# A decoder layer on one core: the queries and keys of its second attention normed and rotated in pairs

## The chip, the cores and the metric

The kernel runs on one core of a Trainium2 chip. The metric is the device time of one launch, in microseconds. Before the change, three runs took 2617.15, 2618.02 and 2619.67 us, median 2618.02 us.

## The reference, cut to what matters

One layer of a decoder: a retention attention, a layer norm, a second attention over a long context and the own tokens, a layer norm, a gated feed-forward, a layer norm. All is float32. There are 8 batches of 100 tokens, the model is 1024 wide, the context has 722 tokens per batch. The change concerns the first lines of the second attention:

```python
q = (x @ wq).reshape(B, L, NUM_HEADS, HEAD_DIM)      # 16 heads of 128
k = (x @ wk).reshape(B, L, NUM_KV_HEADS, HEAD_DIM)   # 4 heads of 128
v = (x @ wv).reshape(B, L, NUM_KV_HEADS, HEAD_DIM)
q = rms_norm(q, q_norm_w)      # q * rsqrt(mean(q*q) + eps) * w
k = rms_norm(k, k_norm_w)
...
q = q * cos + rotate_half(q) * sin    # rotate_half: concat([-x2, x1])
k = k * cos + rotate_half(k) * sin
k_full = jnp.concatenate([k_ctx, k], axis=1)
...
out = jnp.einsum('bhlm,bmhd->blhd', probs, v_full)
```

## The kernel before, in words

**Layout.** Features lie on the 128 partitions, tokens along the columns. The 800 tokens are worked in two halves of 400 columns (4 batches of 100). A float32 number is split in two parts, hi and lo (`split2`, lines 68 to 70: ACT copies hi, DVE subtracts to get lo), and each product is three matmuls (`mm3`, lines 87 to 90: hi by hi, hi by lo, lo by hi). A projection (`proj`, line 102) is 8 k tiles of three matmuls, 24 in all, into one bank of PSUM. Banks have tags: three of "a", four of "s", one of "v"; the projections of this stage take "a" and "s" by turns (`acc_tag`).

**Stages.** First the retention attention (from line 308), then its output projection and layer norm (`out_proj`, whose result z1 is made half by half), then the stage of the change (lines 397 to 424), then the attention over the context (from line 427, "big", "kall" and "kss" are tiles of it), its output projection, and the feed-forward.

**The stage of the change.** A loop over four kv heads; each has four blocks of queries (i = 0 to 3), one of keys (4) and one of values (5), loaded as weights in groups of two to four (`load_w`, line 72: a DMA, an ACT cast and a DVE subtraction of 1024 columns). Every block is projected for both halves: 48 projections, 40 of them queries and keys. For such a one, lines 413 to 423 do:

- the square of the accumulator (ACT, tile sq, L414);
- its sum over the partitions, on GpSimd (`all_red`, L125, a PARTITION_ALL_REDUCE from sq to ss);
- the rotation (`rope`, lines 128 to 138) on DVE: the accumulator by the cosines (L134, from PSUM), the upper and the lower 64 partitions by the sines, written to the other half (L135, L136, both from PSUM), and the sum (L137);
- the inverse root (`inv_root`, lines 112 to 121): logarithm, exponential and square on ACT (L115, L116, L118) and two steps on DVE (L119, L120);
- the scaling by it (DVE, L419), and the split (ACT L69, DVE L70) to d, from which a DMA of 400 KB stores it in DRAM (L423).

Values are copied by ACT (vt, L143), transposed by TensorE (L146), split and stored. The accumulator's bank is free when L414 and L134 to L136 have read it.

**What sets the order.** All instructions of an engine run in one order, waiting by semaphores. The order is made when the program is built: a scheduler that follows a model of the engines' times places each instruction on its engine, so that operations of neighbouring projections are interleaved. All DMAs here are issued from SP's queue, also in one order. Pools give the tiles of the stage two buffers (three for d, one for vs and vt); a tile waits until its buffer has been read.

Of the kernel before, what the change touches and what calls it, by code (L numbers as in the profile page):

```python
# [8 lines left out]
F32 = mybir.dt.float32  # L9
# [7 lines left out]
P = 128  # L17
B, T, D = 8, 100, 1024
NB = 4                 # batches in a half
N = NB * T             # tokens in a half  # L20
KT = D // P            # k tiles of the model width
QT = KT // 2           # k tiles in one of the four big tiles
SC, SH = 722, 362      # context tokens per batch, and in the first half of it
SN = [SH, SC - SH]
NC = 7                 # chunks of keys: SC of the context, then T own ones
ORDER = (6, 5, 0, 1, 2, 3, 4)
C5 = SC - 5 * P        # context keys in chunk 5
R6 = SC + T - 6 * P    # keys in chunk 6
T6 = T - R6            # first token that sees keys of chunk 6
N6 = 4 * R6            # scores of chunk 6, of the tokens that see its keys  # L30
NH1 = 8                # heads of the first attention
NKV = 4                # kv heads of the second
NHID = 32              # blocks of the hidden width
UNITS = NHID // 2      # pairs of hidden blocks
LAST = 3               # pairs of the last down projection
CUT = 5 * T            # tokens in the first of the two parts that are normed last
# [5 lines left out]
def decoder_layer(ctx, tc, xT, cT, w1, wo1, w2, wo2, wc, w3, wd, gw, qw, kw, trig, dec, mask, out):  # L42
# [21 lines left out]
    def split(dst, src):  # L64
        """dst[:, 0] + dst[:, 1] == src, each with the 12 significant bits that one pass takes."""
        split2(dst[:, 0], dst[:, 1], src)
# [44 lines left out]

    def inv_root(pool, ss, eps, n=N):
        """-2 (ss + eps)^-1/2: by exp(-ln/2), then a Newton step."""
        r = pool.tile([P, n], F32, tag="r0", name="r0")
        nc.scalar.activation(r, ss, AF.Ln, bias=eps)  # L115
        nc.scalar.activation(r, r, AF.Exp, scale=-0.5)  # L116
        q = pool.tile([P, n], F32, tag="r1", name="r1")
        nc.scalar.activation(q, r, AF.Square)  # L118
        nc.vector.scalar_tensor_tensor(q, ss, eps, q, ALU.add, ALU.mult)  # L119
        nc.vector.scalar_tensor_tensor(q, q, 3.0, r, ALU.subtract, ALU.mult)  # L120
        return q
# [6 lines left out]
    def rope(pool, acc, cosw, sinw, tag="t1"):  # L128
        """acc * cos + (acc with its halves swapped) * sin."""
        t1 = pool.tile([P, N], F32, tag=tag, name=tag)  # L130
        t2 = pool.tile([P, N], F32, tag="t2", name="t2")
        a = bt(acc)
        h = P // 2
        nc.vector.tensor_tensor(bt(t1), a, cosw[:, None, :].to_broadcast([P, NB, T]), ALU.mult)  # L134
        nc.vector.tensor_tensor(bt(t2[0:h]), a[h:P], sinw[h:P, None, :].to_broadcast([h, NB, T]), ALU.mult)  # L135
        nc.vector.tensor_tensor(bt(t2[h:P]), a[0:h], sinw[0:h, None, :].to_broadcast([h, NB, T]), ALU.mult)  # L136
        nc.vector.tensor_tensor(t1, t1, t2, ALU.add)  # L137
        return t1

    def tokens_first(pool, acc):  # L140
        """[128, 4 x 100] -> PSUM [100, 4 x 128]: the transposes of the four batches."""
        vt = pool.tile([P, N], F32, tag="vt", name="vt", bufs=1)
        nc.scalar.copy(vt, acc)  # L143
        tr = bank("s")
        for b in range(NB):
            nc.tensor.transpose(tr[0:T, b * P:(b + 1) * P], vt[:, b * T:(b + 1) * T], ident)  # L146
        return tr[0:T]

# [1 line left out]
    o1d = dr.tile([NH1, P, 2, 2, 2, N], FR, name="o1d")            # head, p, half, block, hi/lo, token  # L150
# [42 lines left out]
    def load_constants(p, trg):  # L193
# [6 lines left out]
        # rotary tables with the norm weights of q and k; factors left over from inv_root  # L200
# [3 lines left out]
        nc.vector.tensor_scalar(tk, trg[:, 2:4], wts[:, 3:4], None, ALU.mult)  # L204
        return dcy

# [1 line left out]
    def out_proj(half, w, load_o, res, yp, ybufs, p, make_z, dst, after=None):  # L208
        """res + o @ w of one half, then its layer norm: split for the next products, and to dst."""
# [71 lines left out]
    # A norm with little left to do once the last block of rows is there: all blocks are taken relative to the mean  # L281
    # of the others, so that the mean of what they then hold, delta, is that of the last block alone, and the
    # variance is mean(y^2) - delta^2 (delta^2 is at most an eighth of mean(y^2)).
# [24 lines left out]
    with sbuf("l1", 2) as p:  # L308
# [17 lines left out]
        for h in range(NH1):  # L326
# [14 lines left out]
            # scores with their decay, and o^T  # L341
# [21 lines left out]
            # a block of the context weights, split once for all batches  # L363
# [33 lines left out]
    kapool = sbuf("ka", 2, "right")  # L397
    ka = kapool.__enter__()
    with sbuf("l2", 2) as p:
        for kv in range(NKV):  # L400
            for i0, i1 in ((0, 4), (4, 6)) if kv == 0 else ((0, 2), (2, 4), (4, 6)):
                ws = [load_w(w2[kv, i]) for i in range(i0, i1)]
                for half in range(2):
                    bs = slice(half * NB, (half + 1) * NB)
                    for i in range(i0, i1):
                        acc = proj(ws[i - i0], z1[half], tag=acc_tag())
                        if i == 5:
                            tr = tokens_first(p, acc).rearrange("p (b d) -> p b d", b=NB)
                            vs = p.tile([T, NB, 2, P], FR, tag="vs", name="vs", bufs=1)
                            split2(vs[:, :, 0], vs[:, :, 1], tr)  # L410
                            nc.sync.dma_start(out=f32(vd[kv, :, bs]), in_=f32(vs))
                            continue
                        sq = p.tile([P, N], F32, tag="sq", name="sq")
                        nc.scalar.activation(sq, acc, AF.Square)  # L414
                        ss = all_red(p, sq, "ss")
                        tb = tq if i < 4 else tk
                        t = rope(p, acc, tb[:, 0], tb[:, 1])
                        r = inv_root(p, ss, eps_k)
                        nc.vector.scalar_tensor_tensor(  # L419
                            t, t, -0.5 if i < 4 else -0.5 * math.sqrt(P), r, ALU.mult, ALU.mult)  # L420
                        d = p.tile([P, NB, 2, T], FR, tag="d", name="d", bufs=3)
                        split2(d[:, :, 0], d[:, :, 1], bt(t))
                        nc.sync.dma_start(out=f32(qd[kv, i, :, bs] if i < 4 else kd[kv, :, bs]), in_=f32(d))  # L423
    z1pool.__exit__(None, None, None)

# [1 line left out]
    y2pool = sbuf("y2", 1)  # L427
    y2p = y2pool.__enter__()
    with sbuf("cx", 2) as p, sbuf("c1", 1) as p1:
        for b in range(B):  # L430
# [10 lines left out]
            for kv in range(NKV):  # L441
                # K^T of the context, to be scaled by its norms when the scores leave PSUM, and V
# [29 lines left out]
                # -2 / norm of the context keys, keys on partitions  # L472
# [14 lines left out]
                # scores, keys on partitions, and their maximum  # L487
# [23 lines left out]
                # exponentials, split, and their sum  # L511
# [27 lines left out]
                # 1 / sum: exp(-ln), then a Newton step (the sum is 1 or more)  # L539
# [22 lines left out]
    # [C11 C12; C21 C22] = [A11 A12; A21 A22] [B11 B12; B21 B22] by Strassen's seven products; the rows of A  # L562
    # are two blocks of one weight, the columns of B the two halves of the tokens
# [60 lines left out]
    def w_pair(*ops):  # L624
        """Two of the sums of quarters of a weight, split; a sum goes to the first quarter's place unless that is kept."""
# [15 lines left out]
    def seven(i, part, t0=None):  # L641
        """Two blocks of the gate (part 0) or of the other factor (part 1): C11, C12, C21, C22."""
# [24 lines left out]
        add(s2, s2, s4)                                     # C21  # L667
# [6 lines left out]
        add(s4, s4, prod(t2, 1, "b11+b12"))                 # C22  # L674
        m5 = prod(t3, 0, "b22")
        add(s1, s1, m5, ALU.subtract)                       # C11
        add(s3, s3, m5)                                     # C12
        return s1, s3, s2, s4

    # the first two blocks by all eight products: half of them need the first half of the tokens alone  # L680
# [13 lines left out]
    with sbuf("ff", 1) as p:  # L694
# [59 lines left out]
        # the last rows are normed in two parts  # L754
# [16 lines left out]
def _chunks(w, n):  # L771
    """[K, M] -> [M / 128, K / (n 128), 128, n 128]: k tiles of 128 x 128 side by side."""
    import numpy as np
    K, M = w.shape
    a = w.reshape(K // (n * P), n, P, M // P, P)
    return np.ascontiguousarray(a.transpose(3, 0, 2, 1, 4)).reshape(M // P, K // (n * P), P, n * P)
# [62 lines left out]
```

## Time and profile before

| what | value |
|---|---|
| median of three runs | 2618.02 us |
| span of the profiled execution | 2615.0 us |
| TensorE matmul busy | 2552.7 us, 98% |
| DVE busy | 1922.2 us, 74% |
| ACT busy | 1256.3 us, 48% |
| GpSimd busy | 466.3 us, 18% |
| mean granted TensorE clock | 0.992 |
| L125, all-reduce of sq to ss, 56 times (40 in the stage) | 157.3 us, 2817 ns mean |

The profile is of one execution. Its own time is its span, from the first to the last instruction, 2615.0 us; the runs that are timed without it lie 2.2 to 4.7 us above. The page divides the span in 40 slices of 65.4 us and gives a digit per slice, the busy share in tenths. Lines such as "L137 DVE TENSOR_TENSOR t<-t,t" name the line of the kernel, the engine, the operation, and the tiles written and read; then come how many there are, their busy time, the mean of one in ns, and the idle time of the engine ahead of them with what ended it. "PE" is TensorE's matmul, "PEld" its weight load.

### The profile page before, as it was taken

The numbers are of one execution on the slowest core, as the hardware profiler recorded it, in microseconds if no ns is written. First come the engines' busy times: TensorE is split into PE (matmuls) and PEld (weight loads), VectorE is DVE, ScalarE is ACT, GpSimd is POOL, SyncE is SP. The second block draws the span as 40 slices with busy tenths as digits, with TensorE's granted clock in tenths as the row PEclk, the third lists the DMA queues.
The fourth block names the chain that finished last, engine by engine and source line by source line (L and its number), as shares of the span: only waits on it lengthen the run. The fifth ranks groups of instructions, "written<-read, shape, count | busy, mean of one in ns | idle before, by whom it ended". The sixth has DMA issues, their size and how long they took to land.

```text
span 2615.0 us, 37589 instructions
## 1 busy us (share of the span) xinstructions
PE 2552.7 (98%) x14438; PEld 2511.4 (96%) x14438; DVE 1922.2 (74%) x3201; ACT 1256.3 (48%) x2202; POOL 466.3 (18%) x222
## 2 busy tenths in 40 slices
PE   8999999999998899999999999999999999999998
PEld 8999999999998899999999999999999999999996
DVE  4454554456999888888988989866866766866885
ACT  4555544533555455655655566533433433423351
POOL 0010000000544434434333343100000000000000
PEclk9999999999999999999999999999999999999999
DMA  5323333664434644544554553564421211211221
GB/s 173 98 98 119 100 117 122 214 241 154 144 133 138 236 158 137 188 158 146 174 166 139 185 173 113 210 245 143 146 73 65 73 57 65 81 50 64 70 84 51
DMA packets 157233, 346.44 MB, mean 132 GB/s; under 512 B 45018, under 2 KB 95578, under 8 KB 147838
## 3 DMA queue, kind: packets, MB, share of 16 engines
q1 hardware_dynamic: 157054, 344.05, 39.5%
q8 instruction: 113, 1.85, 0.3%
q14 instruction: 66, 0.54, 0.1%
HBM read 279.81 MB, written 64.19 MB: 132 GB/s over the span
## 4 chain that ended last, share of the span: by engine, by line
PE 80%; DVE 10%; ACT 6%; issue 3%; DMA 2%; SPq 0%; DVEq 0%; ACTq 0%
PE a L88 16%; PE a L90 16%; PE a L89 16%; PE s L88 8%; PE s L89 8%; PE s L90 8%; PE v L88 3%; PE v L90 2%; PE v L89 2%; DVE r L119 1%; ACT L116 1%; ACT L115 1%; PE s L469 1%; DVE ot L378 1%; DVE t L136 1%
## 5 line engine op out<-in xcount | busy, mean ns | idle before, releaser
L88 PE MATMUL a<-big,w 128*128 128x400 f32 (+2 forms) x2300 | 778.5, 339 | 17.1 <-ACT big L69 9.5
L89 PE MATMUL a<-big,w 128*128 128x400 f32 (+2 forms) x2300 | 779.7, 339 | 0.0
L90 PE MATMUL a<-big,w 128*128 128x400 f32 (+2 forms) x2300 | 778.3, 339 | 0.0
L88 PEld LDWEIGHTS a<-big,w 128*128 128x128 f32 x2300 | 432.4, 188 | 20.6 <-ACT big L69 9.8
L90 PEld LDWEIGHTS a<-big,w 128*128 128x128 f32 x2300 | 433.9, 189 | 0.6
L89 PEld LDWEIGHTS a<-big,w 128*128 128x128 f32 x2300 | 433.1, 188 | 1.1 <-DVE big L70 0.5
L69 ACT CAST w<-wst 128x1024 fp32r<-128x1024 f32 (+2 forms) x300 | 259.2, 869 | 346.6 <-PE a L90 152.6
L70 DVE TENSOR_TENSOR w<-wst,w 128x1024 fp32r<-128x1024 f32 (+2 forms) x300 | 303.7, 1015 | 164.8 <-ACT w L69 163.2
L125 POOL PARTITION_ALL_REDUCE ss<-sq x56 | 157.3, 2817 | 725.4 <-DVE sq L362 442.3
L459 POOL PARTITION_ALL_REDUCE kss<-ksq x64 | 171.6, 2682 | 141.2 <-ACT ksq L458 140.7
L69 ACT CAST w<-as 128x512 fp32r<-128x512 f32 x90 | 55.9, 621 | 215.3 <-PE a L90 180.9
L88 PE MATMUL s<-big,w 128*128 128x400 f32 x428 | 150.4, 352 | 2.5 <-ACT big L69 2.5
L89 PE MATMUL s<-big,w 128*128 128x400 f32 x428 | 149.4, 349 | 1.6 <-DVE big L70 1.6
L90 PE MATMUL s<-big,w 128*128 128x400 f32 x428 | 148.8, 348 | 0.0
L505 ACT ACTIVATE s<-s,rk 128x400 f32<-128x400 f32 x160 | 88.0, 591 | 97.3 <-DVE sm L527 63.3
L663 DVE TENSOR_TENSOR s<-s 128x400 f32<-128x400 f32 x183 | 102.4, 569 | 25.3 <-ACT s L659 19.5
L125 POOL PARTITION_ALL_REDUCE mb<-sm x32 | 83.3, 2603 | 201.1 <-DVE sm L527 201.1
L524 ACT ACTIVATE s<-s 128x800 f32<-128x800 f32 (+1 forms) x128 | 95.1, 750 | 41.0 <-DVE s L518 38.1
L70 DVE TENSOR_TENSOR pl<-s,ph 128x800 fp32r<-128x800 f32 (+1 forms) x128 | 108.3, 850 | 2.5 <-ACT ph L69 2.0
L506 DVE TENSOR_TENSOR mx<-mx,s 128x400 f32<-128x400 f32 x128 | 80.5, 629 | 26.5 <-ACT s L505 23.3
L88 PE MATMUL a<-z,w 128*128 128x400 f32 x192 | 70.5, 367 | 24.0 <-DVE t L136 22.9
L69 ACT CAST ph<-s 128x800 fp32r<-128x800 f32 (+1 forms) x128 | 92.4, 731 | 0.9
(269 smaller groups left out, 5605.6 us busy)
## 6 DMA issues: line engine op xcount, KB each, us to landing
wst<-in_w SPq DMA_DIRECT2D x137, 512.0 KB
w<-wcd SPq DMA_DIRECT2D x64, 1024.0 KB
wst<-in_wo SPq DMA_DIRECT2D x64, 512.0 KB
wst<-in_wd SPq DMA_DIRECT2D x32, 512.0 KB
o1d<-of SPq DMA_DIRECT2D x32, 400.0 KB
big<-o1d SPq DMA_DIRECT2D x16, 800.0 KB
qd<-d SPq DMA_DIRECT2D x32, 400.0 KB
q<-qd SPq DMA_DIRECT2D x32, 400.0 KB
```

The source lines that it names most:

```text
L69: nc.scalar.copy(hi, src)
L70: nc.vector.tensor_tensor(lo, src, f32(hi), ALU.subtract)
L88: nc.tensor.matmul(acc, lh, rh, start=start, stop=False)
L89: nc.tensor.matmul(acc, lh, rl, start=False, stop=False)
L90: nc.tensor.matmul(acc, ll, rh, start=False, stop=stop)
L115: nc.scalar.activation(r, ss, AF.Ln, bias=eps)
L125: nc.gpsimd.partition_all_reduce(y, x, P, op)
L459: nc.gpsimd.partition_all_reduce(ss[:, at], sq[:, at], P, RED.add)
L505: nc.scalar.activation(sc, sp, AF.Copy, scale=rk[:, c:c + 1])
L506: nc.vector.tensor_tensor(mx, s[:, 1] if j == 2 else mx, sc, ALU.max)
L524: nc.scalar.activation(e, e, AF.Exp)
L663: nc.vector.tensor_tensor(t, x, y, op)
```

## The change

The function `rope` is no longer used in this stage. A new function `normed` takes two projections at once: two query blocks of the same half of the tokens, or the two halves of the key block. The square and the product with the cosines are still made per projection, straight from PSUM; the swap of the halves is now two ACT copies of 64 partitions from PSUM to t2. All that follows works on 800 columns: the sum over the partitions, the product with the sines, the sum, the inverse root, the scaling and the split. For this the rows of the sine tables are swapped once at the start. Tiles sq, d, r0 and r1 of this stage have one buffer, ss, t1 and t2 two. The keys of both halves are stored by one DMA in place of two; for each query block there is one, as before. The order of loops and weights is as before, but that the keys of both halves come ahead of the first values. Comments were dropped as well, which shifts line numbers.

```diff
-    def inv_root(pool, ss, eps, n=N):
+    def inv_root(pool, ss, eps, n=N, bufs=None):
...
         nc.vector.tensor_scalar(tk, trg[:, 2:4], wts[:, 3:4], None, ALU.mult)
+        for t in (tq, tk):
+            sw = p.tile([P, T], F32, tag="sw", name="sw", bufs=1)
+            nc.vector.tensor_copy(sw, t[:, 1])
+            nc.vector.tensor_copy(t[0:P // 2, 1], sw[P // 2:P])
+            nc.vector.tensor_copy(t[P // 2:P, 1], sw[0:P // 2])
...
     with sbuf("l2", 2) as p:
+        def wide(tag):
+            return p.tile([P, 2, N], F32, tag=tag, name=tag, bufs=1 if tag == "sq" else 2)
+
+        def normed(accs, cosw, sinw, scale):
+            sq, t1, t2 = wide("sq"), wide("t1"), wide("t2")
+            h = P // 2
+            for i, acc in enumerate(accs):
+                acc = acc()
+                nc.scalar.activation(sq[:, i], acc, AF.Square)
+                nc.scalar.copy(t2[0:h, i], acc[h:P])
+                nc.scalar.copy(t2[h:P, i], acc[0:h])
+                nc.vector.tensor_tensor(bt(t1[:, i]), bt(acc), cosw[:, None, :].to_broadcast([P, NB, T]), ALU.mult)
+            ss = wide("ss")
+            nc.gpsimd.partition_all_reduce(ss, sq, P, RED.add)
+            b4 = t2.rearrange("p i (b t) -> p (i b) t", b=NB)
+            nc.vector.tensor_tensor(b4, b4, sinw[:, None, :].to_broadcast([P, 2 * NB, T]), ALU.mult)
+            nc.vector.tensor_tensor(t1, t1, t2, ALU.add)
+            flat = lambda t: t.rearrange("p i n -> p (i n)")
+            r = inv_root(p, flat(ss), eps_k, 2 * N, bufs=1)
+            nc.vector.scalar_tensor_tensor(flat(t1), flat(t1), scale, r, ALU.mult, ALU.mult)
+            d = p.tile([P, 2, NB, 2, T], FR, tag="d", name="d", bufs=1)
+            d4 = d.rearrange("p i b l t -> p (i b) l t")
+            split2(d4[:, :, 0], d4[:, :, 1], t1.rearrange("p i (b t) -> p (i b) t", b=NB))
+            return d
...
-                        sq = p.tile([P, N], F32, tag="sq", name="sq")
-                        nc.scalar.activation(sq, acc, AF.Square)
-                        ss = all_red(p, sq, "ss")
-                        tb = tq if i < 4 else tk
-                        t = rope(p, acc, tb[:, 0], tb[:, 1])
-                        r = inv_root(p, ss, eps_k)
-                        nc.vector.scalar_tensor_tensor(
-                            t, t, -0.5 if i < 4 else -0.5 * math.sqrt(P), r, ALU.mult, ALU.mult)
-                        d = p.tile([P, NB, 2, T], FR, tag="d", name="d", bufs=3)
-                        split2(d[:, :, 0], d[:, :, 1], bt(t))
-                        nc.sync.dma_start(out=f32(qd[kv, i, :, bs] if i < 4 else kd[kv, :, bs]), in_=f32(d))
+                    if i0 < 4:
+                        for j in range(i0, i1, 2):
+                            d = normed([lambda i=i: proj(ws[i - i0], z1[half], tag=acc_tag()) for i in (j, j + 1)],
+                                       tq[:, 0], tq[:, 1], -0.5)
+                            for i in range(2):
+                                nc.sync.dma_start(out=f32(qd[kv, j + i, :, bs]), in_=f32(d[:, i]))
+                        continue
+                    if half == 0:
+                        d = normed([lambda half=half: proj(ws[0], z1[half], tag=acc_tag()) for half in range(2)],
+                                   tk[:, 0], tk[:, 1], -0.5 * math.sqrt(P))
+                        nc.sync.dma_start(out=f32(kd[kv]).rearrange("p b l t -> p (b l t)"),
+                                          in_=f32(d).rearrange("p i b l t -> p (i b l t)"))
```

More of the change, by code (lines that the diff above doesn't have):

```diff
@@ L110, in ln_exp @@
         tc.keep_in_program_order(nc.scalar.preload_act_table_set(LN_EXP))
-    def inv_root(pool, ss, eps, n=N):
-        r = pool.tile([P, n], F32, tag="r0", name="r0")
+    def inv_root(pool, ss, eps, n=N, bufs=None):
+        r = pool.tile([P, n], F32, tag="r0", name="r0", bufs=bufs)
         nc.scalar.activation(r, ss, AF.Ln, bias=eps)
         nc.scalar.activation(r, r, AF.Exp, scale=-0.5)
-        q = pool.tile([P, n], F32, tag="r1", name="r1")
+        q = pool.tile([P, n], F32, tag="r1", name="r1", bufs=bufs)
         nc.scalar.activation(q, r, AF.Square)
@@ L404, in decoder_layer @@
                     bs = slice(half * NB, (half + 1) * NB)
[L405 to L412, printed above, removed]
-                        sq = p.tile([P, N], F32, tag="sq", name="sq")
-                        nc.scalar.activation(sq, acc, AF.Square)
-                        ss = all_red(p, sq, "ss")
-                        tb = tq if i < 4 else tk
-                        t = rope(p, acc, tb[:, 0], tb[:, 1])
-                        r = inv_root(p, ss, eps_k)
-                        nc.vector.scalar_tensor_tensor(
-                            t, t, -0.5 if i < 4 else -0.5 * math.sqrt(P), r, ALU.mult, ALU.mult)
-                        d = p.tile([P, NB, 2, T], FR, tag="d", name="d", bufs=3)
-                        split2(d[:, :, 0], d[:, :, 1], bt(t))
-                        nc.sync.dma_start(out=f32(qd[kv, i, :, bs] if i < 4 else kd[kv, :, bs]), in_=f32(d))
@@ L424, in decoder_layer @@
+                    tr = tokens_first(p, proj(ws[1], z1[half], tag=acc_tag())).rearrange("p (b d) -> p b d", b=NB)
+                    vs = p.tile([T, NB, 2, P], FR, tag="vs", name="vs", bufs=1)
+                    split2(vs[:, :, 0], vs[:, :, 1], tr)
+                    nc.sync.dma_start(out=f32(vd[kv, :, bs]), in_=f32(vs))
     z1pool.__exit__(None, None, None)
```

## The prediction

> **What bounds the kernel now.** First the page's 40 slices, to find the stage. The change touches the queries and keys of the second attention, which the records of tile d place at 671 to 904 us: slices 10 to 13, counted from 0.
>
> ```profile
> PE   8999999999998899999999999999999999999998
> DVE  4454554456999888888988989866866766866885
> PEclk9999999999999999999999999999999999999999
> ```
>
> TensorE is at 90% or more nearly everywhere, but not in slices 12 and 13, and there DVE is at 9. Next the busy time by stretches: TensorE's time and matmuls first, then TensorE loads, DVE, ACT and POOL, then the clock.
>
> ```profile
> 680.00:700.00 20.00, 15.26 (x71) 14.58 (x70) 19.73 (x36) 11.62 (x24) 12.06 (x5) 0.83 0.36 129
> 700.00:720.00 20.00, 20.00 (x113) 19.94 (x112) 19.66 (x33) 10.01 (x20) 8.33 (x3) 1.00 0.49 161
> 720.00:760.00 40.00, 37.36 (x199) 36.97 (x198) 39.51 (x61) 21.64 (x42) 18.97 (x7) 0.96 0.35 125
> 760.00:800.00 40.00, 40.00 (x223) 39.94 (x223) 39.44 (x56) 20.02 (x38) 18.76 (x7) 1.00 0.42 138
> 800.00:840.00 40.00, 32.94 (x169) 32.46 (x168) 39.55 (x58) 20.49 (x38) 17.13 (x7) 0.87 0.42 140
> 840.00:880.00 40.00, 30.95 (x161) 30.30 (x161) 39.65 (x61) 24.68 (x47) 18.09 (x8) 0.94 0.58 203
> ```
>
> DVE is full (98 to 99%), ACT at 54%. TensorE did 936 matmuls in these 200 us; at the pace of 760 to 800 (223 in 40 us) they take 168 us, so **32 us of TensorE are lost here**. The waits say to whom:
>
> ```profile
> PE a L88 <- DVE t L136: 22.9, 5, 7.1
> ```
>
> Five gaps, 22.9 us: a projection wants a PSUM bank that DVE has not read out (L136 is its last reader). The other 9 us are the half clock after gaps (means of 0.83 to 0.96). So DVE sets the pace of this stage. Its groups there (640 to 910 us), busy and mean ns of one:
>
> ```profile
> L137 DVE TENSOR_TENSOR t<-t,t 128x400 f32<-128x400 f32 x40 | 31.0, 777 | 0.1
> L119 DVE SCALAR_TENSOR_TENSOR r<-ss,eps_k,r 128x400 f32<-128x400 f32 x40 | 30.7, 767 | 0.1
> L419 DVE SCALAR_TENSOR_TENSOR t<-t,r 128x400 f32<-128x400 f32 x40 | 30.2, 758 | 0.4
> L70 DVE TENSOR_TENSOR w<-wst,w 128x1024 fp32r<-128x1024 f32 x21 | 30.2, 1443 | 1.6 <-ACT w L69 1.4
> L70 DVE TENSOR_TENSOR d<-t,d 128x400 fp32r<-128x400 f32 x40 | 27.3, 684 | 1.6 <-ACT d L69 1.2
> L135 DVE TENSOR_TENSOR t<-s,tq 64x400 f32<-64x400 f32 x16 | 9.2, 576 | 0.2
> ```
>
> Undisturbed, the timeline has 0.565 us (L137), 0.63 (L119), 0.57 (L419, d) and 1.22 (w). The excess is 8.4 + 5.5 + 7.4 + 4.6 + 4.5 = **30 us in which DVE was blocked**. By what, the timeline shows:
>
> ```profile
> 726.49 2.86 POOL L125 PARTITION_ALL_REDUCE ss<-sq  x1 [1.34 <-DVE r L119]
> 726.81 2.10 DVE L419 SCALAR_TENSOR_TENSOR t<-t,r 128x400 f32<-128x400 f32 x1
> ...
> 731.14 2.60 POOL L125 PARTITION_ALL_REDUCE ss<-sq  x1 [1.79 <-DVE r L119]
> 731.54 0.58 DVE L135 TENSOR_TENSOR t<-s,tq 64x400 f32<-64x400 f32 x1
> 732.15 1.16 DVE L70 TENSOR_TENSOR d<-t,d 128x400 fp32r<-128x400 f32 x1
> ```
>
> L419 takes 2.10 instead of 0.57 us under an all-reduce; L135, which reads PSUM, isn't touched; d is held until about 732.74 (end less 0.57), 1.6 us after the all-reduce began. So one all-reduce of 400 columns closes DVE for 1.6 of its 2.60 us to operations with both inputs in SBUF.
>
> [...]
>
> **The change, part by part.** 40 query and key projections become 20 pairs. Spacings from start to start count, since neighbours overlap (timeline of 725 to 735 us).
> - Before, DVE per projection: L134 0.58, L135 0.61, L136 0.60, L137 0.48, L119 0.55, L120 0.49, L419 0.49, split 0.49, together 4.29; per pair 8.58 us.
> - After: two cosine products from PSUM, 2 x 0.58; sine product, sum, L120's step, scaling and split at 800 columns, 5 x 0.90 (the spacing of L522); L119's step 0.55 + 0.41 = 0.96. Together 6.62. **Saved: 1.96 x 20 = 39 us.** Most of it is the swap of halves (2.42 per pair on DVE), replaced by one 800-column product.
> - ACT: per pair before 2 x (0.49 + 0.62 + 0.53 + 0.54 + 0.53) = 5.4; after 2 x 0.49, four 64x400 copies, 0.96 for the logarithm, 3 x 0.87 (L524 at 128x800). The copies from PSUM appear nowhere in this form: nearest is L143 (128x400, PSUM) at 0.49; bounds 0.39 (its spacing) and 0.60; taken 0.48. Sum 6.5: 21 us more ACT in a stage where it is at 54%, so about 64%. Its load hides; without that cover it would cost those 21 us.
> - POOL: 40 all-reduces of 400 columns become 20 of 800, and nothing in the trace has that size. L459's 362 and 360 columns take 2.38 to 2.46 us against 2.60 for 400: 0.14 to 0.22 us per 38 columns. So 800 take 4.1 to 4.9 us, their lock 1.6 + 1.5 to 2.3 us. Bounds: 1.6 (it doesn't grow) and 4.2 (whole instruction doubled, 5.2, less the 1.0 us tail). I take 3.2: [...]
> - How much of it hits DVE: 30 of 40 x 1.6 = 64 us before, since L134 to L136 (1.79 us) often ran under the lock. After, only 1.16 of 6.62 us per pair read PSUM, and the order of the built program puts the sine product first after the ACT copies, which follow the square that starts the all-reduce. So I take 2.5 of 3.2 us: 50 us, **20 us more than before**. Bounds 15 (lock 1.6, the same share, 47%) and 84 (4.2, all of it).
> - Waits: the sine product now heads DVE's queue and waits for ACT; behind it are the previous pairs' split, L119's step and both cosine products, which free the banks. The banks are "a" 3 and "s" 4, a new projection needs one about every 4.4 us, so a bank may be held some four projections, about 17 us. Some 6 us of delay (lock and three 0.9 us operations) is covered. Without that cover each pair would stop TensorE.
> - ACT's split cast waits for the scaling on DVE, and behind it stand the next squares, and the copy ahead of v's transposes, on which TensorE waits in order. In the built order one or two projections (4.4 us each) lie between; I cost it at nothing, up to 4 us for each of 8 v projections.
> - d, sq, r0 and r1 have one buffer: the next split waits for the previous pair's stores. A pair lasts 9 to 11 us; nothing.
> - DMAs: 32 query stores remain, key stores go from 8 to 4: 1.3 us of SP issue less, which has slack. Weight loads stand behind the stores in SP's queue as before, and their splits stay several pairs ahead of use.
> - The table's swap: six small DVE copies at the start, where DVE is at 63% and TensorE's order hardly changes: nothing, at most 1.3 us.
> - Outside this stage the built order is the same, but for a few matmuls and loads changing places.
>
> Sum: -39 + 20 = **-19 us**. Check: DVE's demand before is 40 x 4.29 + 24 weights x 1.14 + 5 (vs) + 7 (big) + 30 = 241 us, and the trace has 660.6 to 903.7, 243. After it is 222. TensorE needs 48 projections x 24 x 0.179 = 206 us and about 6 for the transposes. DVE stays the bound, by 10 us, and 13 of the 32 lost us stay lost. The next stage is TensorE's, so an earlier end stays won. The page gives the profiled execution's span as 2615.0; the median of the runs is 2618.0, 3.0 more, and the step is taken from it: 2618 - 19 = 2599.
>
> **Rivals.**
> 1. TensorE becomes the bound. If the locks fall on cosine products and DVE's idle time (15 to 30 us in all), all 32 us return: 2586. For it: TensorE works ahead during v projections, which need little DVE. Against: five of every six us per pair now have two SBUF inputs.
> 2. A wait takes the place of the old one: ACT's queue, held by the split cast, delays v's transposes by the 4 us of the bound: 8 x 4 = 32 us. In these stops DVE catches up, so the 13 us at the banks vanish, and 32 are lost as before: 2618. For it: ACT gets more work and more waits on DVE. Against: today that wait is 0.6 us on TensorE.
> 3. Slower: the 800-column all-reduce closes DVE longer. It decides where the block per pair passes (39 + 30) / 20 = 3.5 us. At the bound of 4.2 us, all of it hitting, DVE's sum is -39 + 54 = +15, and gaps bring more half clock: about 2633. For it: nothing here shows 800 columns. Against: the slope of the three sizes gives 3.1 to 3.9, and not all hits.
>
> **How the numbers follow.** Forecast (2590 to 2608) 0.45; rival 1 0.20; rival 2 0.13; rival 3 0.22. 0.2% is 5 us, about what a measurement of this kernel can tell from no change. Faster: 0.45 + 0.20 = 0.65; same 0.13; slower 0.22. The range runs from 2584 (all lost time back, 2 us spare) to 2622, the near end of rival 3; beyond it lie some 0.17 above and 0.03 below.
>
> **What would show it.** All-reduces near 4.2 us, each holding one DVE operation for 2 to 3 us; DVE still at 95% or more; the waits for banks down from 22.9 to about 10; tile d ending near 883 instead of 904. It is wrong if the all-reduce is over 5 us, if TensorE waits for vt, or if the gain sits outside this stage.

## The result, and the profile after

| | before | after |
|---|---|---|
| median of 20 runs each, same chip | 2616.68 us (2613.28 to 2620.59) | 2620.39 us (2617.84 to 2623.18) |
| span of the profiled execution | 2615.0 us | 2618.1 us |

The ratio is 1.0014 [1.0008, 1.0021]: the kernel became a little slower, where 2599 had been forecast. The change does what it says, but the stage takes as long as it did: the last record of tile d ends at 908.2 us, before at 903.7.

The slices of the kernel after, to be held against those of before:

```profile
PE   8999999999889999999999999999999999999998
DVE  4454554456899878889889989866866766866885
PEclk9999999999999999999999999999999999999999
```

TensorE still has its two poor slices; they have moved from 12 and 13 to 10 and 11. DVE had 9, 9, 9, 8, 8 in slices 10 to 14 and now has 8, 9, 9, 8, 7: it is a little less full, and TensorE isn't better fed for it. The stretches of the kernel after (TensorE, its loads, DVE, ACT, POOL, then the clock):

```profile
680.00:700.00 20.00, 14.89 (x82) 14.26 (x81) 19.07 (x14) 11.37 (x19) 10.88 (x2) 0.99 0.33 120
700.00:720.00 20.00, 16.92 (x86) 16.84 (x87) 18.58 (x19) 14.56 (x25) 9.25 (x2) 0.84 0.42 148
720.00:760.00 40.00, 38.27 (x209) 37.70 (x207) 39.31 (x33) 27.66 (x43) 19.86 (x5) 1.00 0.36 130
760.00:800.00 40.00, 33.13 (x174) 33.04 (x175) 33.77 (x32) 24.12 (x38) 13.96 (x4) 0.87 0.41 144
```

Between 760 and 800 us, TensorE's best stretch before (223 matmuls), both engines now stand idle for a part of it: 174 matmuls, and DVE at 33.8 of 40 us. The waits of the kernel after (us in total, times, longest):

```profile
ACT r L115 <- DVE r L120: 40.6, 14, 5.4
...
PE s L146 <- ACT vt L143: 20.2, 3, 7.4
...
PE a L88 <- DVE t L418: 9.4, 3, 7.8
DVE d L70 <- ACT d L69: 8.1, 8, 1.9
...
DVE t L418 <- ACT t L417: 6.0, 7, 1.7
```

The stops for a bank went from 22.9 to 9.4 us, as forecast. In their place TensorE stands 20.2 us, in three stops, at the transposes of v, for ACT's copy (0.6 us before). DVE now waits for ACT: 8.1 us for the split's cast (1.2 before) and 6.0 for the swapped copies. DVE's groups of the kernel after, busy and mean ns:

```profile
L120 DVE SCALAR_TENSOR_TENSOR r<-r,r 128x800 f32<-128x800 f32 x20 | 53.4, 2670 | 0.1
L422 DVE TENSOR_TENSOR t<-t,tq 128x800 f32<-128x800 f32 x16 | 32.8, 2049 | 0.0
...
L426 DVE SCALAR_TENSOR_TENSOR t<-t,r 128x800 f32<-128x800 f32 x20 | 22.9, 1143 | 0.1
L70 DVE TENSOR_TENSOR d<-t,d 128x800 fp32r<-128x800 f32 x20 | 21.4, 1069 | 8.2 <-ACT d L69 8.1
```

An operation on 800 columns takes 0.98 us undisturbed (L522 of the kernel before, at 128x800, has 0.975 in the median), and 0.91 from start to start (L426 and L422 of the kernel after, at 862.30 and 863.21), where 0.90 had been forecast. L120 and L422 have the same size and take 2.67 and 2.05 on average: the lock of the all-reduce now falls mostly on these two. One pair, from the timeline of the kernel after, shows the whole chain:

```profile
758.60 4.85 POOL L420 PARTITION_ALL_REDUCE ss<-sq  x1 [6.01 <-DVE r L119]
758.83 4.15 DVE L120 SCALAR_TENSOR_TENSOR r<-r,r 128x800 f32<-128x800 f32 x1
...
763.07 0.96 ACT L115 ACTIVATE r<-ss,eps_k 128x800 f32<-128x800 f32 x1 [2.58 <-DVE r L120]
...
764.81 0.86 ACT L69 CAST d<-t 128x800 fp32r<-128x800 f32 x1 [0.78 <-DVE t L426]
765.58 0.86 ACT L116 ACTIVATE r<-r 128x800 f32<-128x800 f32 x1
766.35 0.47 ACT L143 COPY vt<-s 128x400 f32<-128x400 f32 x1
...
766.87 1.09 PE L146 MATMUL s<-ident,vt 128*100 128x128 f32 x4 [7.39 <-ACT vt L143]
```

The all-reduce begins at 758.60; L120, 0.98 us of work, ends at 762.98, so DVE was let in at 762.00: the lock, from the start of the all-reduce to there, is 3.4 us of the 4.85. ACT stands behind L120 (r0 has one buffer), then behind the scaling; only at 766.35 does it copy v out of its bank, and TensorE, idle for 7.4 us, goes on at 766.87. One lock is thus passed on through DVE and ACT to TensorE. It isn't the whole stop: of the 7.4 us, ACT stands idle for 3.4 (2.58 and 0.78), and the other 4.0 are its own instructions that the order puts ahead of the copy, and the copy.

For the experiments one number is taken from each trace: **blocked time**, the durations of the DVE instructions between 660 and 912 us less what the same size takes undisturbed (0.57 us for 400 columns, 0.905 for the 720 and 724 of tile big, 0.985 for 800, 1.22 for 1024), where that excess is over 0.25 us. It is 30.7 us before and 58.7 after, good to about 1 us; in these two kernels every instruction that it counts overlaps an all-reduce.

### The profile page after: what moved, and what is told of

Read it like the earlier page. It is cut to its first block, busy times and chain, and to the rows that moved or that the text cites. A ratio compares the mean times of both kernels' runs of the same rounds, so it can differ in the third digit from the quotient of the medians.

```text
span 2618.1 us, 37344 instructions
## 1 busy us (share of the span) xinstructions
PE 2550.3 (97%) x14438; PEld 2510.2 (96%) x14438; DVE 1910.1 (73%) x3047; ACT 1285.7 (49%) x2202; POOL 465.1 (18%) x202
## 4 chain that ended last, share of the span: by engine, by line
PE 81%; DVE 9%; ACT 5%; issue 3%; DMA 2%; POOL 0%; SPq 0%; DVEq 0%; ACTq 0%; POOLq 0%
PE a L88 16%; PE a L90 16%; PE a L89 16%; PE s L88 8%; PE s L89 8%; PE s L90 8%; PE v L88 3%; PE v L90 2%; PE v L89 2%; DVE r L120 2%; DVE w L70 1%; DVE r L119 1%; PE s L498 1%; ACT L116 1%; ACT L115 1%
## 5 line engine op out<-in xcount | busy, mean ns | idle before, releaser
L88 PEld LDWEIGHTS a<-big,w 128*128 128x128 f32 x2300 | 433.4, 189 | 19.2 <-ACT big L69 9.2
L420 POOL PARTITION_ALL_REDUCE ss<-sq x20 | 108.3, 5417 | 284.8 <-DVE z L70 165.6
L125 POOL PARTITION_ALL_REDUCE ss<-sq x16 | 43.7, 2730 | 442.4 <-DVE sq L367 442.4
L125 POOL PARTITION_ALL_REDUCE mb<-sm x32 | 83.3, 2603 | 197.5 <-DVE sm L556 197.5
```

What stands on the lines that cost most here:

```text
L88: nc.tensor.matmul(acc, lh, rh, start=start, stop=False)
L125: nc.gpsimd.partition_all_reduce(y, x, P, op)
L420: nc.gpsimd.partition_all_reduce(ss, sq, P, RED.add)
```

## The experiments

Theory: the lock that an all-reduce puts on DVE is what the stage loses, before and after; the change took out of DVE's work the products from PSUM, which can run under the lock (L135 kept its 0.58 us there), and left what can't (L419 took 2.10 us for 0.57). Rival A: the single buffers of r0, r1, sq and d. Rival B: ACT's longer queue, by way of v's transposes. The expectations name them by these causes. One reservation holds for all: only pool_later keeps nearly the order of instructions of the kernel after. In the others the scheduler laid the stage out anew, so no run changes one thing with the order held fixed. Ratios are to the kernel before, on the same chip.

| kernel | median us | ratio [95%] | blocked us |
|---|---|---|---|
| before_no_reduce | 2585.92 | 0.9878 [0.9864, 0.9891] | 2.8 |
| no_reduce | 2583.56 | 0.9868 [0.9855, 0.9881] | 2.6 |
| half_reduce | 2592.98 | 0.9902 [0.9889, 0.9916] | 20.0 |
| ones_sum_before | 2594.65 | 0.9911 [0.9898, 0.9925] | 2.8 |
| ones_sum | 2596.65 | 0.9927 [0.9913, 0.9940] | 1.3 |
| two_reduces | 2608.66 | 0.9966 [0.9952, 0.9979] | 47.7 |
| late_v_two_reduces | 2614.35 | 0.9991 [0.9985, 0.9998] | 41.5 |
| two_buffers_two_reduces | 2616.06 | 0.9997 [0.9989, 1.0005] | 43.1 |
| swap_alone | 2617.76 | 0.9996 [0.9988, 1.0004] | 51.0 |
| pair_alone | 2619.98 | 1.0006 [0.9998, 1.0015] | 32.2 |
| two_buffers | 2621.86 | 1.0017 [1.0009, 1.0024] | 54.4 |
| pool_later | 2622.05 | 1.0014 [1.0008, 1.0021] | 58 |
| late_v_but_last | 2625.15 | 1.0026 [1.0015, 1.0037] | 56.3 |
| late_v | 2628.43 | 1.0047 [1.0035, 1.0060] | 57.7 |
| vt_on_dve | 2632.25 | 1.0055 [1.0041, 1.0068] | 59.7 |
| extra_reduce | 2649.18 | 1.0121 [1.0105, 1.0136] | 79.9 |

### The single buffers: two_buffers and pool_later

```diff
-            return p.tile([P, 2, N], F32, tag=tag, name=tag, bufs=1 if tag == "sq" else 2)
+            return p.tile([P, 2, N], F32, tag=tag, name=tag, bufs=2)
...
-            r = inv_root(p, flat(ss), eps_k, 2 * N, bufs=1)
+            r = inv_root(p, flat(ss), eps_k, 2 * N, bufs=2)
...
-            d = p.tile([P, 2, NB, 2, T], FR, tag="d", name="d", bufs=1)
+            d = p.tile([P, 2, NB, 2, T], FR, tag="d", name="d", bufs=2)
```

To make room, the pool "ka" of the next stage is opened after this one; pool_later does only that.

> The changed kernel with two buffers for r0, r1, sq and d in the pair stage (room for them is made by opening the pool of tile kall after the stage). Theory 1, ACT's queue: the logarithm L115 waits for L120 because r0 has one buffer, L120 is held by the all-reduce, and the copy to vt stands behind it, so TensorE stops at the values' transposes. Then the wait of L115 for L120 (40.6 us) goes, the gaps at the transposes (20.2 us) fall under 5, and the time is about 2600. Theory 2, the lock: all-reduces now block DVE for some 58 us in place of 30, DVE's demand is as large as before, and buffers only move the loss to waits for banks: 2613 to 2621.

> Control: the changed kernel with the pool of tile kall opened after the pair stage, nothing else. Both theories: as the changed kernel, 2617 to 2624, with the gaps at the transposes still there.

pool_later is the kernel after, within its interval, and two_buffers gains nothing over it. The wait of L115 for L120 is gone, as it should be, but ACT now stands at the next step instead. The waits of two_buffers:

```profile
ACT d L69 <- DVE t L422: 42.3, 15, 5.3
...
PE s L146 <- ACT vt L143: 15.9, 5, 5.2
PE a L88 <- DVE kall L488: 8.2, 1, 8.2
...
ACT ksq L485 <- DMA vd<-vs: 6.5, 1, 6.5
```

40.6 us behind L120 became 42.3 behind the scaling: a buffer doesn't help an engine whose next input is late anyway. So nothing is left of rival A's gain of 20 us, but the test isn't clean. The stop of 8.2 us at the first keys of the next stage hangs on ACT's wait for the last store of v. The likely reason, not tested, is that the pool opened later takes over the memory of this stage; pool_later itself shows no such stop. Without it, two buffers might win some 8 us.

### The lock: no_reduce, two_reduces, half_reduce, extra_reduce

```diff
 no_reduce
-            nc.gpsimd.partition_all_reduce(ss, sq, P, RED.add)
+            ss = sq
 two_reduces
-            nc.gpsimd.partition_all_reduce(ss, sq, P, RED.add)
+            for i in range(2):
+                nc.gpsimd.partition_all_reduce(ss[:, i], sq[:, i], P, RED.add)
 extra_reduce (pool_later and this)
+            sx = p.tile([P, N], F32, tag="sx", name="sx", bufs=1)
+            nc.gpsimd.partition_all_reduce(sx, sq[:, 0], P, RED.add)
```

In half_reduce one all-reduce of 400 columns, of the first projection's squares, serves both projections of a pair.

> The changed kernel without the all-reduces of the pair stage: the squares are used in place of their sum over the partitions, so that part of the norm is left out. Theory 2: the 58 us of blocked DVE go, DVE falls under TensorE's need, and nearly all of TensorE's lost time comes back: 2586 to 2592. Theory 1 in its strong form, in which the single buffers alone hold ACT: the wait of L115 for L120 stays, and the time stays above 2605.

> The changed kernel with two all-reduces of 400 columns per pair in place of one of 800. Theory 2: what counts is the length of one block; two of 1.6 us can fall apart and on products from PSUM, so blocks fall from 58 towards 40 us and the time to about 2608. Theory 1: L115 still waits for L120 and the copy to vt is still behind it: 2615 to 2622.

> The changed kernel in which one all-reduce of 400 columns serves a pair: the second projection of each pair is normed with the sums of the first, so part of the norm is left out. Buffers, and who waits for whom, stay. Theory of the lock: at most 20 x 1.6 = 32 us can be blocked; between no all-reduce (2583.6) and two of 400 (2608.7): 2588 to 2600. Theory of ACT's queue: the wait of L115 for L120 stays, above 2605.

> pool_later with one more all-reduce of 400 columns per pair, of the first half of the squares, whose result nobody reads: more lock, and the same work on every other engine. If the blocked DVE time sets the stage, 20 more locks of 1.6 us block some 20 to 30 us more and the time rises by 12 to 30 us over pool_later's 2622: 2634 to 2652. If the lock isn't what costs, GpSimd has room (its all-reduces fill less than half of the stage) and the time stays within 2618 to 2626.

The time follows the lock both ways: with none of it 2583.6, with half of it 2593.0, with one more that nobody reads 2649.2, 27 us over pool_later for 22 us more blocked. (no_reduce came out 2 us below its forecast, two_reduces with 48 us blocked for 40.) Leaving an all-reduce out also takes away the time for which its result is awaited, and no run parts the two; but extra_reduce adds one whose result nobody awaits, and ACT's waits for GpSimd at sq stay as they are (5.2 us, 4.9 in pool_later). In no_reduce TensorE never stands; two of its stretches, where the kernel after had 86 and 174 matmuls:

```profile
700.00:720.00 20.00, 20.00 (x113) 19.95 (x112) 18.35 (x23) 17.36 (x27) 0.00 (x0) 1.00 0.57 195
...
760.00:800.00 40.00, 40.00 (x222) 40.00 (x221) 35.14 (x41) 34.38 (x52) 0.00 (x0) 1.00 0.41 134
```

ACT is at 34.4 of 40 us in the second, fuller than in the kernel after (24.1), and v's copies are in time. This speaks against rival B: the same work on ACT, with the same single buffers, delays nobody once DVE isn't held. Nor do ACT's waits for L120 cost by themselves: in half_reduce they are still 30.7 us, and TensorE stops for 7.3. That two_reduces wins 12 us says that the size of the all-reduce counts too, with the swap on ACT: two locks of 400 columns, the first of which can begin a projection earlier, block 48 us instead of 59.

### The change in halves: swap_alone and pair_alone

swap_alone is the kernel before with this in `rope`'s place, and the sine rows swapped as in the kernel after; pair_alone is the kernel after with the swap by DVE:

```diff
 swap_alone, per projection
+        nc.scalar.copy(t2[0:h], acc[h:P])
+        nc.scalar.copy(t2[h:P], acc[0:h])
+        nc.vector.tensor_tensor(bt(t1), bt(acc), cosw[:, None, :].to_broadcast([P, NB, T]), ALU.mult)
+        nc.vector.tensor_tensor(bt(t2), bt(t2), sinw[:, None, :].to_broadcast([P, NB, T]), ALU.mult)
 pair_alone
-                nc.scalar.copy(t2[0:h, i], acc[h:P])
-                nc.scalar.copy(t2[h:P, i], acc[0:h])
+                nc.vector.tensor_tensor(bt(t2[0:h, i]), bt(acc)[h:P], sinw[h:P, None, :].to_broadcast([h, NB, T]), ALU.mult)
+                nc.vector.tensor_tensor(bt(t2[h:P, i]), bt(acc)[0:h], sinw[0:h, None, :].to_broadcast([h, NB, T]), ALU.mult)
```

> The kernel before with the swap of halves by ACT copies alone, one projection at a time (400 columns, one all-reduce of 400 for each). Theory of the lock: DVE saves 29 us of work (0.61 + 0.60 - 0.49 on 40 projections), but the two products taken away read PSUM and ran under the lock; with 0.58 us left that do, blocks rise from 30 to about 46 us: net -13, about 2605. Theory of ACT's queue: 40 us of copies more on ACT and more waits before vt, but no 800-column steps and two buffers: if only single buffers did the harm, the 29 us come back in full: about 2589.

> The changed kernel with the swap made on DVE from PSUM, as before, so pairing alone: sums, inverse roots, scaling and splits at 800 columns, all-reduces of 800. Theory of the lock: DVE's own work falls by 9 us (0.44 a pair), and 3.6 us per pair read PSUM and may run under a lock of 3.4 us: blocks between 30 and 45 us, in place of 58: 2609 to 2619. Theory of ACT's queue: the single buffer of r0 is still there, so the gaps at the transposes stay as in the changed kernel and the time is 2619 to 2626.

Neither changes the time measurably, and swap_alone is a miss for both theories: 2617.8, where the lock had been forecast at about 2605 and the queue at 2589. pair_alone, at 2620.0, lies just above the range of the lock and in that of the queue, but the stops at the transposes, which by the queue should have stayed at 20.2 us, are 9.7. DVE's 250 us from 660 to 910 divide so (busy from the stretches, own work = busy less blocked, idle = the rest):

| kernel | own work | blocked | idle |
|---|---|---|---|
| before | 207.0 | 30.7 | 12.3 |
| swap_alone | 179.8 | 51.0 | 19.2 |
| pair_alone | 197.9 | 32.2 | 19.9 |
| after | 168.7 | 58.7 | 22.6 |

The three must add up to 250, whatever the kernel; what the table tells is into what the saved work turned. The swap alone takes 27 us of work from DVE and gives 20 of them to the lock, with all-reduces of the same 400 columns in the same number; the other 7 become idle time, which the forecast of 2605 had put at nothing. The blocked share of the lock shows why. 40 locks of 1.6 us are 64 us; before, 48% of that blocked DVE, with the swap on ACT 80%. 20 locks of 3.4 us are 68 us; with the swap on DVE 47% of it blocked, in the kernel after 86%. So the larger all-reduce alone doesn't raise the blocked time (by 1.5 us in pair_alone); on top of the swap it adds 8 (51.0 to 58.7). The main part comes with L135 and L136, which ran under the lock without harm (576 and 568 ns on average, L135 at 731.54 under an all-reduce 0.58 us) and are gone. The traces show it: the products from PSUM fill some 28 us of the locks' time before and 35 in pair_alone, but 9 in swap_alone and 5 in the kernel after (each lock counted as 1.6 or 3.4 us from the start of its record). One row of the kernel before and the same of swap_alone:

```profile
L120 DVE SCALAR_TENSOR_TENSOR r<-r,r 128x400 f32<-128x400 f32 x41 | 23.7, 579 | 0.6
...
L120 DVE SCALAR_TENSOR_TENSOR r<-r,r 128x400 f32<-128x400 f32 x41 | 39.8, 971 | 0.1
```

The same step on the same 400 columns takes 579 ns before and 971 with the swap on ACT: it has moved under the lock.

### ACT's queue and v's transposes: vt_on_dve, late_v, late_v_but_last

```diff
 vt_on_dve
-        nc.scalar.copy(vt, acc)
+        (copy or nc.scalar.copy)(vt, acc)
...
+                    tr = tokens_first(p, proj(ws[1], z1[half], tag=acc_tag()), nc.vector.tensor_copy).rearrange("p (b d) -> p b d", b=NB)
 late_v (pool_later and this)
-                    tr = tokens_first(p, proj(ws[1], z1[half], tag=acc_tag())).rearrange("p (b d) -> p b d", b=NB)
...
+                    late.append((kv, bs, copied_v(p, proj(ws[1], z1[half], tag=acc_tag()))))
...
+                        if half == 1:
+                            flush()
 late_v_but_last (late_v and this; vs with two buffers)
+                    if kv == NKV - 1:
+                        flush()
```

`copied_v` is ACT's copy to vt, with two buffers; `flush` does the transposes, the split and the store of the values kept in `late`. It comes after the first query pairs of the next kv head.

> The changed kernel with the values' copy from PSUM to vt on DVE in place of ACT, in this stage. Theory of the lock: TensorE's stops at the transposes go or move, but DVE's demand is the same plus 8 copies of 0.5 us, so the loss turns up as waits for banks or in DVE's queue: 2615 to 2625. Theory of ACT's queue: the 20 us at the transposes come back: 2598 to 2606.

> The kernel after, with one thing moved: v's copy keeps its place, but its transposes, its split and its store come after the next query pairs, so that TensorE has at least three more projections to do while ACT gets to the copy (v's copy has two buffers for that, and the pool of the next stage's keys opens later). If the 20 us of stops at v's transposes are a cost of their own, they go and the time falls by 10 to 18 us, to about 2603 to 2611, with the waits of transposes for vt near 0. If the blocked DVE time alone sets the stage, the same time is lost at the banks instead: 2616 to 2622, the waits of projections for a bank up from 9 to about 20 us, the blocked time still 54 to 60 us.

> late_v with two things put right: the last v keeps its transposes where they were, since behind it no query pair is left to hide them, and v's split has two buffers, so that ACT doesn't stand before a store. If the stops at v's transposes cost by themselves, what late_v lost at its end (9 us at the last transposes, 9 us at the first keys of the next stage) comes back and the time is 2603 to 2612. If they are only where the blocked DVE time shows, it is 2616 to 2622 again, with TensorE's stops of 25 to 35 us at banks and at the next stage's first keys, and 54 to 60 us blocked.

With the copy on DVE the kernel is 12 us slower than after, slower than either forecast. TensorE still waits 17.2 us for the copy, now on DVE, whose queue is the late one. With the transposes three projections later, two of the three stops at v are gone (those of 7.4 and 6.3 us that the kernel after has at 767 and 829 us). The third, at the last v, grows from 6.5 to 9.1 and 12.0 us, and for the rest TensorE stands at banks and at the first keys of the next stage. Its waits in late_v_but_last:

```profile
PE s L439 <- ACT vt L142: 12.0, 1, 12.0
PE s L88 <- DVE t L419: 10.2, 3, 5.1
PE a L88 <- DVE kall L508: 3.0, 1, 3.0
PE a L88 <- ACT vt L142: 2.0, 1, 2.0
PE a L88 <- DVE t L419: 1.3, 2, 0.9
```

All stops together are 29.2 us from 660 to 930 (after: 30.1), and 56.3 us are blocked. Neither kernel gains; I expected 2603 to 2612 if the stops were a cost of their own, and 2616 to 2622 if only blocked time counts. They took 2628 and 2625, so both forecasts missed, and why they are slower than after stays open; part of it can be the stop at the next stage's first keys (9.3 us in late_v), where ACT waits for a store of v as in two_buffers. That the total of the stops stays speaks for a delay that only arrives at the transposes and comes from elsewhere. Not all of rival B could be removed, since at the last v nothing is left to be put ahead.

### Does the saved work pay where there is no lock? before_no_reduce

```diff
-                        ss = all_red(p, sq, "ss")
+                        ss = sq
```

> The kernel before with the sum over the partitions left out in this stage: each value is normed with its own square. It shows what the change is worth where there is no lock: no_reduce, the same with the change, took 2583.6. By the terms of the sum, DVE's demand before falls from 241 to 211 us and meets TensorE's 212, so 2584 to 2592: the change would then be worth 0 to 8 us. If the work that the change takes off DVE (39 us) sets the time even without a lock, it is above 2600.

Without the lock the kernel before takes 2585.9 us, the changed one 2583.6, with overlapping intervals. DVE's work was left as it is, some 38 us a stage more than after, and nearly all the time that TensorE lost in this stage comes back (it stands for 1.7 us). From 760 to 800 us, in before_no_reduce:

```profile
760.00:800.00 40.00, 40.00 (x222) 40.00 (x221) 38.90 (x70) 23.75 (x46) 0.00 (x0) 1.00 0.46 155
```

DVE is at 97% and TensorE at 100%: full, but in time. DVE's own work costs at most a few microseconds here; the all-reduces, with the lock and the waits for their results, cost 32 before (2617.4 to 2585.9) and 37 after (2620.4 to 2583.6).

### Versions that keep the sum: ones_sum, ones_sum_before, and the pairs with two_reduces

```diff
 ones_sum (ones_sum_before: the same in the kernel before)
-            nc.gpsimd.partition_all_reduce(ss, sq, P, RED.add)
+            for i in range(2):
+                sm = bank("v")[:, :N]
+                nc.tensor.matmul(sm, ones, sq[:, i], start=True, stop=True)
+                nc.scalar.copy(ss[:, i], sm)
```

`ones` is a 128x128 matrix of ones, and sq is written as fp32r, the type of the split parts. late_v_two_reduces and two_buffers_two_reduces join the edits of their names.

> The kernel after, with the sum of the squares over the partitions by TensorE: the squares are written in the reduced fp32 format, a matrix of ones times them gives each column's sum in every partition, and ACT copies it out of PSUM. GpSimd does nothing in this stage. If the lock of the all-reduce is what cost the gain, the blocked DVE time falls to 3 us as in no_reduce, and the time is no_reduce's 2583.6 plus 40 matmuls of 0.18 us, plus some for the copies (40 of 0.49 us on ACT): 2588 to 2598. If ACT's longer queue is what costs (it has 20 us more to do here), the transposes wait for vt for more than 20 us and the time stays above 2610.

> The kernel before with the sum over the partitions by TensorE, as in ones_sum (which took 2596.65): no all-reduce in this stage, queries and keys one projection at a time, the swap of halves on DVE. DVE's demand of 211 us is under TensorE's 212 + 7: 2590 to 2600, within 5 us of ones_sum, if removing the lock is the whole gain of that kernel; above 2605 if the change's part in it counts.

> The same, and the sum over the partitions by two all-reduces of 400 columns instead of one of 800. If both are costs of their own, the gains add: two_reduces gave 12 us, so 2593 to 2602. If blocked DVE time alone decides, it ends where two_reduces did, at 2606 to 2611.

> two_buffers with two all-reduces of 400 columns. Blocked time alone: as two_reduces, 2606 to 2611, since the second buffers brought nothing. If the single buffers are a cost that the longer lock hid, they show now: below 2603.

Both kernels with ones beat the kernel before, by 20.7 and 22.7 us, and stand 9 to 13 above their versions without any sum: 40 more matmuls at 0.179 us are 7.2 of these. Between them the change makes no difference, [0.9898, 0.9925] without it and [0.9913, 0.9940] with it. The whole gain comes from the all-reduces being gone.

The two joined kernels are misses. Less is blocked in them than in two_reduces (42 and 43 us against 48), yet they are 6 and 7 us slower. In both, TensorE waits 7.3 us at a bank as the next stage begins, and two_reduces, whose pool opens early, shows no such stop. Behind it ACT waits 6.5 and 6.2 us for the last store of v, as in two_buffers. That stop has the size of the difference, but no run takes it away. So blocked time orders the large effects between kernels with the same work on DVE, and not differences of under some 8 us; what sets those isn't shown.

## Why the prediction was wrong, by its steps

The step that failed is the one from DVE's saved work to time: "-39 + 20" takes work off DVE as if all of it came back but 20 us. Blocked time rose by 28 us instead of 20, DVE's idle time, put at nothing, by 10, and TensorE's stops at v's transposes, put at nothing, to 20.2 us. The 2620 us lie in the forecast's widest range (2584 to 2622), but on the other side of the time before.

- **The bound.** "DVE sets the pace of this stage" was right about the engine and wrong about what of it. I read 98% busy as work, had counted 30 us of it as blocked, and still took the work as the lever. before_no_reduce shows that nearly the whole loss goes with the all-reduces, the work left as it is. (One digit was misread: DVE is at 9 in slice 12 but at 8 in slice 13; nothing hangs on it.)
- **DVE's own work, saved 39 us.** Right: 207.0 to 168.7 is 38.
- **ACT.** The copies take 0.485 to 0.490 us (taken: 0.48), and ACT is at 63% of the window (forecast: 64%). "Its load hides" failed: DVE now waits 8.1 us for the cast and 6.0 for the copies.
- **The all-reduce.** 4.85 us, within 4.1 to 4.9; lock 3.4, taken 3.2. **"So I take 2.5 of 3.2 us: 50 us" is the first failed term**: 58.7 us, 2.9 per pair, 86% of the lock instead of 78%. The direction was seen, that fewer operations read PSUM, but not its weight.
- **The banks.** Covered, as argued: 9.4 us of stops, forecast about 10.
- **v's transposes. "I cost it at nothing, up to 4 us for each" is the second failed term**: 20.2 us in three stops of up to 7.4. "If TensorE waits for vt" was a sign of being wrong that the prediction named itself. With the transposes moved, as much is lost in other stops (29.2 us in all in late_v_but_last, 30.1 in the kernel after); how far the stops depend on the order that was built isn't shown.
- **Single buffers "nothing".** Not refuted, and not settled: the waits are there, 40.6 us on ACT, and two_buffers wins nothing, but with a stop of 8.2 us that its own edit may have brought.
- **The sum.** "DVE's demand ... After it is 222" is the third failed term: it treats DVE as never idle. It was idle 12.3 us before and 22.6 after. So the 38 us saved went to blocked time (28) and idle time (10). In a window of fixed length the three must cancel, so they say where the work went and not what the time became; for that there is the last record of d, at 908.2 us where 883 had been forecast, and the spans, which differ by +3.1. The last 3 us I can't assign. Nor did DVE stay at 95% or more: it is at 91% from 660 to 910.
- **The rivals.** Rival 2 (2618) came nearest, with 20 of its 32 us at the transposes and ACT late. But ACT was held mainly by the logarithm behind L120 (40.6 us), less by the split's cast (12.2), and in no_reduce the same work on ACT delays nobody. Rival 3's point of 3.5 us blocked per pair wasn't reached: 2.9 were enough, as the lock also costs idle time that its price left out.

## What to carry to other kernels

Before work is taken off a full engine, split its busy time into work and blocked time, and ask which instructions lie under the lock now and which will after: removing those that could run there turned saved work into blocked time here (20 of 27 us in swap_alone). An experiment that leaves the blocking instruction out of the unchanged kernel gives the price of that instruction, lock and latency together, in one run, and here it would have shown the 32 us and the right lever. An added wait shouldn't be priced alone: a hold of 3 us on DVE passed to ACT, and with what stood in ACT's queue TensorE stopped for 7.

## What the runs showed of the hardware

- An all-reduce over 128 partitions takes 2.60 us at 400 columns and 4.85 at 800 in its shortest records, and holds DVE's operations with both inputs in SBUF for 1.6 and 3.4 us of these (d at 732.15 of the kernel before, L120 at 758.83 of the kernel after). In the traces before and after, each DVE operation that an all-reduce of 400 columns held was let in 1.00 us before the end of the record, and 1.46 us at 800 columns, also where the record is longer (up to 8.1 us in the kernel after). How exact GpSimd's records are isn't shown.
- DVE's products from PSUM ran at their usual length under the lock (L135, 0.58 us), and taking them away raised the blocked time from 30.7 to 51.0 us with the same all-reduces (swap_alone).
- Behind a stop of 4.16 us (before, at 685.16) TensorE's matmuls of 400 columns start 0.33 us apart, at a granted clock of 0.50, until 690.6, and then 0.18 us apart at 1.00; behind the stop of 7.39 us (after, at 766.87) they do so until 771.4.
- 22 us more blocked in extra_reduce cost 27 us. TensorE's clock is 0.89 to 0.93 in five of its six stretches between 680 and 880 us, where no_reduce, without stops, has 1.00; but from 660 to 910 us extra_reduce has 0.94 and pool_later, too, only 0.93, so the clock isn't shown to be the 5 us.
- The sum over the partitions by ones costs a matmul of 0.18 us (start to start) and a copy of 0.49 on ACT for 400 columns. Hardly anything is blocked (1.3 and 2.8 us), and in ones_sum_before TensorE waits 0.9 us for the copy.
